# A two-layer graph network on one NeuronCore: layer 1 entered tile by tile, its weights prepared during layer 0's experts, key and value scales moved to the context

## The chip, the cores and the metric

One Trainium2 chip, one of its NeuronCores. The metric is device time in microseconds of one execution, median of the runs. A profiled execution of the same program gives busy times, waits and the granted TensorE clock; it is longer than the plain runs, and its own time is given beside its span.

## The reference, cut to what matters

There are 3125 nodes of 256 features and 50,000 edges sorted by destination. Each of two layers adds to the node features x a graph branch and a mixer branch, both computed from the layer norm of x, and then an expert branch. Layer 0 ends with eight experts of which each node uses two. Layer 1 is:

```python
xn = _layernorm(x)
x = x + gnn1(xn) + mix1(xn)
x = x + ffn1(_layernorm(x))

# mix1, with heads of 32 features
q, k, v = split((xn @ w_qkv + b_qkv) by head)
k = _ln(k, kln_g, kln_b)
v = _ln(v, vln_g, vln_b)
kv = einsum('nhd,nhe->hde', k, v) / 3125
h = gelu((einsum('nhd,hde->nhe', q, kv) + xn) @ w1 + b1)
mix1 = h @ w2 + b2 + xn

# gnn1: mean of xn[src] over the edges of each node
o = concat([xn, agg]) @ weight
gnn1 = o / norm(o) + bias

# ffn1: softmax router over 8 experts, all used; each is
# relu(bn(x W1 + b1)), relu(bn(h W2 + b2)), h Wo + bo
```

All of it is float32.

## The kernel before, in words

The nodes lie in 25 tiles of 128 rows (the last has 53). X (L345) holds all of them in SBUF. Instructions are put in order by a scheduler which starts from the order of the program; each engine then works its own queue strictly in that order. Four kinds of PSUM tile exist, "tr", "mm", "acc" and "seg", with two buffers each (L195).

*Layer 0's experts* (L944 to L973) run over 32 slots of 256 gathered rows. A slot loads its expert's two weights and its rows on SP's DMA queue, transposes, multiplies twice with Gelu between, and writes its result to the DRAM table yex from ScalarE's queue. From slot 8 on, every third slot also issues the loads of one layer-1 expert's three weights (L970).

*Layer 1's beginning* (L978 to L1056). Once the loop is over, the pool lp is opened, the mixer's and the graph branch's weights and seven rows of constants are loaded, and three things are prepared on VectorE: the key and value weights lose their head means (hm, L1001 to L1006, so that keys and values come out centred), the query weights are transposed (wqT), and m_b2 is added to g_bias. Then chunks of four tiles (L1014) are entered: eight gathers from yex on POOL, two weighted adds per tile into X (L1025), layer norm statistics, the normalizing on VectorE (L1030), two transposes, a copy into xT (L1034), a product with half of g_w (L1036) whose result goes to the DRAM table xtab (L1038), and two VectorE instructions that add the normed rows and g_bias to X (L1039, L1040). The edge gathers of layer 1 read xtab and can start once the whole table is stored.

*The mixer* (mixer1, L1062). Per tile: keys and values by a 128x512 product, offset added (L1071), Square on ScalarE, sum by head (L1074), Sqrt on ScalarE, reciprocal, multiplication by the inverse deviation (L1077), by kvln_g (L1079), addition of kvln_b (L1080), and two products that accumulate the context in the two "acc" buffers (L1083). After 25 tiles the diagonal blocks go to cb, are multiplied into w1 and the query weights (L1094 to L1107), and seven chunks of tiles, last tiles first (BACK: six of four tiles and one of one), get the mixer's output added to X.

*The experts of layer 1* (L1154). For each chunk of BACK: route (layer norm, transposes, router, softmax, bias product), then eight experts of two products with Relu and a third product added to X. Routing of the next chunk is begun beside expert 3 or later of the present chunk, if the edge sums of its tiles are complete.

*Order written by hand* (L1262 to L1276). The generator other() yields units of expected TensorE time: 3.7 per tile of keys and values, 6.0 for the context, 0.85 per tile and product pair after that. The 49 groups of eight edge blocks are inserted in between: group g when 14 + 11.5 g units have passed, or at once where an expert chunk waits for them. A group builds a one-hot tile on VectorE (L290), sums eight blocks of 128 edges with one product each (L1241), spreads the sums over node tiles (L1254 to L1258) and, where a node tile is complete, closes it (aggregate, L1196 to L1210), which needs an "acc" buffer.

Of the kernel before, what the change touches and what calls it, by code (L numbers as in the profile page):

```python
# [8 lines left out]
F32 = mybir.dt.float32  # L9
I32 = mybir.dt.int32  # L10
AF = mybir.ActivationFunctionType
ALU = mybir.AluOpType
# [175 lines left out]
def fast_path(ctx: ExitStack, tc: tile.TileContext, i, out, ident, dstP):  # L188
# [750 lines left out]
    fW = [fw.tile([Q, NE, KC, D], F32, name=f"fw_{n}", tag=f"fw_{n}") for n in ("f_W1", "f_W2", "f_Wo")]  # L939
    with ExitStack() as l0e:  # L940
# [3 lines left out]
        for k in range(MT):  # L944
# [24 lines left out]
            nc.scalar.dma_start(yex[k * ME:(k + 1) * ME, :].rearrange("(j p) c -> p j c", p=Q), yo)  # L969
            if k >= 8 and k % 3 == 2 and (k - 8) // 3 < NE:  # L970
                e = (k - 8) // 3
                for w, name in zip(fW, ("f_W1", "f_W2", "f_Wo")):
                    nc.sync.dma_start(w[:, e], i[name][e].rearrange("(k p) c -> p k c", p=Q))  # L973
# [4 lines left out]
    lp = ctx.enter_context(tc.tile_pool(name="lp", bufs=1))  # L978
    wk = ctx.enter_context(tc.tile_pool(name="wk", bufs=2))

    def weights(name, n, k=KC):
        t = lp.tile([Q, k, n], F32, name=f"w_{name}", tag=f"w_{name}")
        nc.sync.dma_start(t, i[name].rearrange("(k p) c -> p k c", p=Q))
        return t

    wqkv = weights("m_wqkv", 3 * D)
    w1 = weights("m_w1", D)
    w2 = weights("m_w2", D)
    wg = weights("g_w", D, 2 * KC)
    wr = weights("f_Wr", NE)  # L990
    fbo = lp.tile([NE, D], F32, name="fbo", tag="fbo")
    nc.sync.dma_start(fbo, i["f_bo"])
    br = row_load(lp, "br")
    kvb = row_load(lp, "kv_b")
    lng = row_load(lp, "kvln_g").rearrange("p (s d) -> p s d", s=2)
    lnb = row_load(lp, "kvln_b").rearrange("p (s d) -> p s d", s=2)
    gb = row_load(lp, "g_bias")
    mb2 = row_load(lp, "m_b2")
    nc.vector.tensor_tensor(gb, gb, mb2, ALU.add)

    hm = lp.tile([Q, KC + 1, 2 * NH], F32, name="hm", tag="hm")  # L1001
    for k in range(KC + 1):
        w = (wqkv[:, k, D:3 * D] if k < KC else kvb).rearrange("p (h d) -> p h d", d=DH)
        nc.vector.tensor_reduce(hm[:, k, :], w, AX.X, ALU.add)
        nc.vector.tensor_scalar(hm[:, k, :], hm[:, k, :], 1.0 / DH, None, op0=ALU.mult)
        nc.vector.tensor_tensor(w, w, bc(hm[:, k, :], 2, DH), ALU.subtract)  # L1006

    wqT = lp.tile([Q, KC, D], F32, name="wqT", tag="wqT")
    for k in range(KC):
        pt = transposed(wqkv[:, k, 0:D])  # L1010
        nc.vector.tensor_copy(wqT[:, :, k * Q:(k + 1) * Q], pt)
    xT = lp.tile([Q, KC, NT, Q], F32, name="xnT", tag="xnT")
    xtab = dram.tile([NPAD, D], F32, name="xtab", tag="xtab")
    for t0, n in CHUNKS:  # L1014
        xs = X[:, t0:t0 + n, :]
        for k in range(2):
            ye = wk.tile([Q, 4, D], F32, name="ye", tag="c4", bufs=7)
            for j in range(n):
                r = rows(t0 + j)
                nc.gpsimd.indirect_dma_start(  # L1020
                    out=ye[0:r, j, :], out_offset=None, in_=yex[:, :],
                    in_offset=bass.IndirectOffsetOnAxis(ap=slot[0:r, k, t0 + j:t0 + j + 1], axis=0))
            for j in range(n):
                r = rows(t0 + j)
                nc.vector.scalar_tensor_tensor(X[0:r, t0 + j, :], ye[0:r, j, :], gate[0:r, k, t0 + j:t0 + j + 1],  # L1025
                                               X[0:r, t0 + j, :], op0=ALU.mult, op1=ALU.add)
        mv, rs = ln_stats(xs, n)
        xn = wk.tile([Q, 4, D], F32, name="xn", tag="c4", bufs=7)
        for j in range(n):
            normed(xn[:, j, :], xs[:, j, :], mv, rs, j)  # L1030
        yt = wk.tile([Q, 4, D], F32, name="yt", tag="c4", bufs=7)
        for j in range(n):
            pt = transposed(xn[:, j, :])
            nc.scalar.copy(xT[:, :, t0 + j, :], pt)  # L1034
            py = ps("seg", [Q, D])
            product(py, [xT[:, k, t0 + j, :] for k in range(KC)], [wg[:, KC + k, :] for k in range(KC)])  # L1036
            nc.scalar.copy(yt[:, j, :], py)
        nc.sync.dma_start(xtab[t0 * Q:(t0 + n) * Q, :].rearrange("(t p) c -> p t c", p=Q), yt[:, 0:n, :])  # L1038
        nc.vector.tensor_tensor(xs, xs, xn[:, 0:n, :], ALU.add)  # L1039
        nc.vector.tensor_tensor(xs, xs, bc(gb, 1, n), ALU.add)  # L1040
# [4 lines left out]

    bn = []
    for s in ("1", "2"):
        g = lp.tile([Q, NE * KC], F32, name=f"bn_s{s}", tag=f"bn_s{s}")
        nc.scalar.activation(g, cols_of("f_v" + s), AF.Sqrt, bias=eps3)
        nc.vector.reciprocal(g, g)  # L1050
        nc.vector.tensor_tensor(g, g, cols_of("f_g" + s), ALU.mult)
        b = lp.tile([Q, NE * KC], F32, name=f"bn_b{s}", tag=f"bn_b{s}")
        nc.vector.tensor_tensor(b, cols_of("f_b" + s), cols_of("f_m" + s), ALU.subtract)
        nc.vector.tensor_tensor(b, b, g, ALU.mult)
        nc.vector.tensor_tensor(b, b, cols_of("f_be" + s), ALU.add)
        bn.append((g, b))  # L1056


    BACK = [list(range(t, max(-1, t - 4), -1)) for t in range(NT - 1, -1, -4)]
    complete = set()  # L1060

    def mixer1():  # L1062

        cx = [ps("acc", [Q, Q]) for _ in range(2)]
        for t in range(NT):
            pm = ps("mm", [Q, 2 * D])
            product(pm, [xT[:, k, t, :] for k in range(KC)], [wqkv[:, k, D:3 * D] for k in range(KC)])
            ks = c4("kv").rearrange("p s (h d) -> p s h d", d=DH)
            kv, sq = ks[:, 0], ks[:, 1]
            kf = kv.rearrange("p h d -> p (h d)")  # L1070
            nc.vector.tensor_tensor(kf, pm, kvb, ALU.add)  # L1071
            nc.scalar.activation(sq, kv, AF.Square)
            va = wk.tile([Q, 2 * NH], F32, name="va", tag="va")
            nc.vector.tensor_reduce(va, sq, AX.X, ALU.add)  # L1074
            nc.scalar.activation(va, va, AF.Sqrt, bias=eps5, scale=1.0 / DH)
            nc.vector.reciprocal(va, va)
            nc.vector.tensor_tensor(kv, kv, bc(va, 2, DH), ALU.mult)  # L1077
            k4 = kv.rearrange("p (s h) d -> p s h d", s=2)
            nc.vector.tensor_tensor(k4, k4, bc(lng, 2, NH), ALU.mult)  # L1079
            nc.vector.tensor_tensor(k4, k4, bc(lnb, 2, NH), ALU.add)  # L1080
            r = rows(t)
            for a in range(2):
                nc.tensor.matmul(cx[a], kf[0:r, D + a * 128:D + (a + 1) * 128], kf[0:r, a * 128:(a + 1) * 128],  # L1083
                                 start=(t == 0), stop=(t == NT - 1))
            yield 3.7
# [907 lines left out]
```

## Time and profile before

| | |
|---|---|
| Median of 3 runs | 2813.36 us (2812.88 to 2814.0) |
| Profiled execution | 2967.99 us, span 2966.2, mean granted clock 0.945 |
| PE | 2640.8 us busy, 89% of the span |
| DVE (VectorE) | 1517.6 us, 51% |
| POOL | 917.0 us, 31% |
| ACT (ScalarE) | 873.5 us, 29% |
| HBM | 160.14 MB read, 53.61 MB written |
| Chain that ended last | PE 79%, DVE 10%, unknown queue 4%, issue 3% |

PE is TensorE, PEld its weight loads, DVE VectorE, ACT ScalarE. One float32 product appears as two MATMUL instructions. Busy time of an engine is the sum of its instructions; idle time of an engine matters only where others wait for it. In a row of instruction groups one reads line, engine, operation, output and inputs, shapes, count, then busy microseconds and mean nanoseconds, then the engine's idle time just before such instructions and what ended it. "Remote", or an unknown queue, is a wait whose end no engine or data transfer in the trace accounts for.

### The profile page before, as it was taken

The page shows a single profiled execution, that of the slowest core. Times are in us where ns is not written, and L with a number is a line of the kernel's source. Part 1 is how long each engine was busy: PE and PEld are TensorE (multiplying, and loading weights), DVE is VectorE, ACT ScalarE, POOL GpSimd, SP SyncE. Part 2 cuts the span into 40 slices and gives each one's busy share as a digit, 9 for nine tenths or more (in the row PEclk, how much of TensorE's full clock was granted, in tenths as well). Part 3 has the DMA queues.
Part 4 walks back from the last instruction along what each step waited for, and adds up shares of the span by engine and source line. Part 5 has one row for each costly group of instructions (what it writes and reads, how often), then busy time and mean ns, then how long its engine had stood idle before and what let it go on. Part 6 is the DMA issues. An engine that isn't in the chain of part 4 may idle for free.

```text
span 2966.2 us, 29959 instructions
## 1 busy us (share of the span) xinstructions
PE 2640.8 (89%) x10578; PEld 1891.9 (64%) x10578; DVE 1517.6 (51%) x3749; ACT 873.5 (29%) x1621; POOL 917.0 (31%) x964
## 2 busy tenths in 40 slices
PE   5899989989988779898998699856789999999998
PEld 4666768656676457686665588734556666666655
DVE  6376655856657557668556311176834333322211
ACT  3432225312252112343333122222233222322223
POOL 2107542144521335200122100065354544555200
PEclk9899999999999889999998799978889999999999
DMA  4002221022212121100111576442122222222100
GB/s 141 12 16 89 81 90 38 22 77 76 86 47 70 29 77 41 59 4 13 31 58 59 191 252 200 153 145 81 47 75 64 75 67 71 71 73 78 33 8 10
DMA packets 152337, 215.85 MB, mean 73 GB/s; under 512 B 21032, under 2 KB 120686, under 8 KB 152178
## 3 DMA queue, kind: packets, MB, share of 16 engines
q1 hardware_dynamic: 104274, 112.31, 11.7%
q0 software_dynamic: 36848, 91.34, 10.8%
q10 hardware_dynamic: 11056, 10.19, 1.1%
q8 instruction: 86, 1.41, 0.2%
q14 instruction: 73, 0.60, 0.1%
HBM read 160.14 MB, written 53.61 MB: 72 GB/s over the span
## 4 chain that ended last, share of the span: by engine, by line
PE 79%; DVE 10%; another core or an unknown queue 4%; issue 3%; ACT 2%; DMA 1%; POOL 0%; SPq 0%; DVEq 0%; ACTq 0%
PE mm L280 33%; PE acc L280 24%; PE seg L467 6%; PE seg L1241 6%; PE acc L614 3%; PE tr L274 3%; PE seg L280 1%; PE acc L335 1%; DVE vals L457 1%; DVE gt L422 1%; DVE st L521 1%; DMA raw<-in_src 0%; PE tr L280 0%; DVE hT L737 0%
## 5 line engine op out<-in xcount | busy, mean ns | idle before, releaser
L283 POOL DMA_INDIRECT gt<-table,srcI x391 | 426.9, 1092 | 807.1 <-DVE m L425 602.9
L283 POOL DMA_INDIRECT gt<-xtab,srcI x391 | 381.7, 976 | 394.8 <-PE seg L1241 241.9
L280 PE MATMUL mm<-hT,w 128*128 128x512 f32 (+2 forms) x896 | 381.7, 562 | 23.7 <-ACT gT L688 16.2
L280 PE MATMUL acc<-w,gT 128*128 128x256 f32 x1600 | 370.0, 387 | 6.2 <-issue 4.2
L280 PEld LDWEIGHTS acc<-w,gT 128*128 128x128 f32 x1600 | 306.4, 194 | 53.1 <-issue 6.9
L1182 ACT ACTIVATE fh<-mm,bn_b,bn_s 128x512 f32<-128x512 f32 (+1 forms) x224 | 163.1, 731 | 425.8 <-PE mm L280 391.9
L280 PEld LDWEIGHTS mm<-hT,w 128*128 128x128 f32 x896 | 164.5, 193 | 158.8 <-issue 100.0
L339 DVE SCALAR_TENSOR_TENSOR X<-acc,rw,X 128x256 f32<-128x256 f32 x200 | 95.1, 483 | 325.9 <-PE acc L280 277.2
L688 ACT ACTIVATE gT<-mm,cols 128x512 f32<-128x512 f32 (+2 forms) x224 | 142.3, 641 | 354.0 <-PE mm L280 263.5
L280 PE MATMUL mm<-wqkv,hT 128*128 128x256 f32 x800 | 214.2, 399 | 15.6 <-ACT hT L723 9.0
L467 PE MATMUL seg<-vals,oh 128*128 128x261 f32 x782 | 192.0, 399 | 13.3 <-DVE oh L290 8.7
L280 PE MATMUL acc<-fw_f_Wo,fh 128*128 128x256 f32 x800 | 198.4, 385 | 1.6 <-issue 0.7
L280 PE MATMUL mm<-fh,fw_f_W 128*128 128x512 f32 (+1 forms) x448 | 195.3, 565 | 1.6 <-ACT fh L1182 1.3
L1241 PE MATMUL seg<-gt,oh 128*128 128x256 f32 x782 | 186.6, 388 | 3.8 <-DVE sum L1258 2.7
L280 PE MATMUL mm<-xc,fw_f_W 128*128 128x512 f32 (+1 forms) x448 | 188.9, 551 | 0.0
L467 PEld LDWEIGHTS seg<-vals,oh 128*128 128x128 f32 x782 | 152.9, 198 | 52.8 <-DVE oh L290 15.7
L280 PEld LDWEIGHTS acc<-fw_f_Wo,fh 128*128 128x128 f32 x800 | 144.7, 190 | 59.1 <-issue 27.9
L1241 PEld LDWEIGHTS seg<-gt,oh 128*128 128x128 f32 x782 | 150.4, 194 | 38.5 <-issue 12.8
L280 PEld LDWEIGHTS mm<-wqkv,hT 128*128 128x128 f32 x800 | 144.2, 197 | 40.4 <-ACT K L566 11.4
L699 DVE TENSOR_TENSOR X<-acc,X 128x256 f32<-128x256 f32 x100 | 42.2, 422 | 220.8 <-PE acc L280 149.2
L1020 POOL DMA_INDIRECT ye<-yex,slot x50 | 51.5, 1030 | 297.4 <-DVE cb L1087 273.8
L280 PEld LDWEIGHTS mm<-fh,fw_f_W 128*128 128x128 f32 x448 | 78.2, 191 | 99.5 <-issue 68.7
(329 smaller groups left out, 3877.0 us busy)
## 6 DMA issues: line engine op xcount, KB each, us to landing
ew<-in_e_W SPq DMA_DIRECT2D x64, 512.0 KB
tok<-zero SPq DMA_DIRECT2D x8, 3328.0 KB
w<-in_W SPq DMA_DIRECT2D x8, 1024.0 KB
hr<-tok SPq DMA_DIRECT2D x32, 256.0 KB
yex<-yo ACTq DMA_DIRECT2D x32, 256.0 KB
gt<-table,srcI POOLq DMA_INDIRECT x391
gt<-xtab,srcI POOLq DMA_INDIRECT x391
fw_f_W<-in_f_W SPq DMA_DIRECT2D x16, 256.0 KB
```

The costliest lines, as they stand in the source:

```text
L274: nc.tensor.transpose(pt[:, k, :], src_row[:, k * Q:(k + 1) * Q], ident)
L280: nc.tensor.matmul(pm, a, b, start=(k == 0), stop=(k == len(lhs) - 1))
L283: nc.gpsimd.indirect_dma_start(out=dst, out_offset=None, in_=tab[:, :], in_offset=bass.IndirectOffsetOnAxis(ap=srcI[:, b:b + 1], axis=0))
L335: nc.tensor.matmul(py, cT[:, j, :], bt, start=True, stop=True)
L339: nc.vector.scalar_tensor_tensor(X[:, t, :], py, cw, X[:, t, :], op0=ALU.mult, op1=ALU.add)
L467: nc.tensor.matmul(open_seg[w_], oh[:, b - h0, :], v[:, b - h0, :], start=(b == a), stop=(b == z))
L614: nc.tensor.matmul(cx[a], K[0:r, t, a * 128:(a + 1) * 128], keys.hn[0:r, t, :], start=(t == 0), stop=(t == NT - 1))
L688: nc.scalar.activation(gT[:, f, :], pm, AF.Gelu, bias=col("b1", l * NF + f))
L699: nc.vector.tensor_tensor(X[:, t, :], py, X[:, t, :], ALU.add)
L1020: nc.gpsimd.indirect_dma_start(out=ye[0:r, j, :], out_offset=None, in_=yex[:, :], in_offset=bass.IndirectOffsetOnAxis(ap=slot[0:r, k, t0 + ...
L1182: nc.scalar.activation(hn[:, a, 0:w], pm, AF.Relu, bias=bn[s][1][:, c:c + 1], scale=bn[s][0][:, c:c + 1])
L1241: nc.tensor.matmul(segs[w], oh[:, j, :], gt[:, j, :], start=(b == z), stop=(b == a))
```

## The change

- Pool lp is opened before the expert loop. The loads and preparations of layer 1's weights become a generator, layer1_weights, advanced at slots 9, 12, 15, 18 and 21 of the expert loop.
- The beginning goes tile by tile. Gathers of both expert results of a tile stand together, in groups of 2, 3 and then 4 tiles; three groups are fetched ahead, and the buffers are those that the edge gathers use later. The tile's adds run four tiles ahead. Both uses of the normalization go to ScalarE: xn, and X + xn as one scaled and shifted copy of X. The addition of g_bias goes to the mixer's output chunks.
- Of the 28 steps of keys and values, 18 are issued among the entries of tiles (three for every four tiles).
- kvln_g and kvln_b no longer touch the keys and values. Scaled values and keys go to a ring of three buffers with a column of ones; the context products give sums of the values beside the context, and one more product with ones per tile gives sums of the keys. At the end scale, offset and their cross terms are applied to the 128x128 context by means of four prepared tiles (cf).
- A remaining step of keys and values counts 2.5 units instead of 3.7.
- BACK becomes four chunks of four tiles and three of three.

```diff
+    def layer1_weights():
+        w = {}
+        w["qkv"] = weights("m_wqkv", 3 * D)
+        w["kvb"] = row_load(lp, "kv_b")
...
+        yield w
...
+    l1w, ready = None, layer1_weights()
...
+            if k >= 9 and k % 3 == 0:
+                l1w = next(ready, l1w)
...
+    BACK = [list(range(t, t - 4, -1)) for t in range(NT - 1, 8, -4)] + [list(range(t, t - 3, -1)) for t in (8, 5, 2)]
...
+    def add_y(t):
...
+        for k in range(2):
+            nc.vector.scalar_tensor_tensor(X[0:r, t, :], yes[g][0:r, 2 * (t - t0) + k, :], gate[0:r, k, t:t + 1],
+                                           X[0:r, t, :], op0=ALU.mult, op1=ALU.add)
+        st = stat.tile([Q, 6], F32, name="st", tag="st", bufs=4)
+        nc.vector.bn_stats(st, X[:, t, :])
+        nc.vector.bn_aggr(mvx[:, t, :], st)
+        if t == t0 + n - 1:
...
+            fetch_y(g + 3)
+    def norm_y(t):
+        xn = wk.tile([Q, D], F32, name="xn", tag="h", bufs=2)
+        nc.scalar.activation(xn, X[:, t, :], AF.Identity, scale=rsx[:, 0, t:t + 1], bias=rsx[:, 1, t:t + 1])
+        pt = transposed(xn)
+        nc.scalar.copy(xT[:, :, t, :], pt)
+        nc.scalar.activation(X[:, t, :], X[:, t, :], AF.Identity, scale=rsx[:, 2, t:t + 1], bias=rsx[:, 1, t:t + 1])
...
+    def keys_values():
+        cx = [ps("acc", [Q, Q + 1]) for _ in range(2)]
+        ks = ps("seg", [Q, 2, Q + 1])
+        def sums(t):
+            kv, r = kvs[t % 3], rows(t)
+            se = dict(start=(t == 0), stop=(t == NT - 1))
+            for a in range(2):
+                nc.tensor.matmul(cx[a], kv[0:r, 2 + a, 0:Q], kv[0:r, a, :], **se)
+            nc.tensor.matmul(ks.rearrange("p a c -> p (a c)"), ones[0:r, :], kv[0:r, 0:2, :].rearrange("p a c -> p (a c)"),
+                             **se)
...
+                nc.vector.tensor_tensor(kvs[t % 3][:, :, 0:Q].rearrange("p g (h d) -> p g h d", d=DH),
+                                        kv.rearrange("p (g h) d -> p g h d", g=4),
+                                        bc(va, 2, DH).rearrange("p (g h) d -> p g h d", g=4), ALU.mult)
+            if t >= 2:
+                sums(t - 2)
+            yield
...
+    AHEAD = 4
+    for t in range(AHEAD):
+        add_y(t)
+    norm_y(0)
+    kvsteps, due = keys_values(), 0
+    for t in range(NT):
+        if t + AHEAD < NT:
+            add_y(t + AHEAD)
+        if t + 1 < NT:
+            norm_y(t + 1)
+        product_y(t)
+        while due < 0.75 * t - 0.5:
+            next(kvsteps)
+            due += 1
+    norms_of_experts()
 
     def mixer1():
...
-            nc.vector.tensor_tensor(kv, kv, bc(va, 2, DH), ALU.mult)
-            k4 = kv.rearrange("p (s h) d -> p s h d", s=2)
-            nc.vector.tensor_tensor(k4, k4, bc(lng, 2, NH), ALU.mult)
-            nc.vector.tensor_tensor(k4, k4, bc(lnb, 2, NH), ALU.add)
...
-            yield 3.7
...
+        for _ in kvsteps:
+            yield 2.5
+        cb = contexts[0]
...
             gT = c4("gT1")
+            nc.vector.tensor_tensor(X[:, t0:t0 + n, :], X[:, t0:t0 + n, :], bc(l1w["gb"], 1, n), ALU.add)
```

The products that product_y issues are those of L1036, unchanged. The two instructions per expert norm at L1046 to L1056 become norms_of_experts, after the last tile is entered.

## The prediction

> **What bounds the kernel now.** I read the stages first: busy time, granted clock and DMA share in five stretches. The borders are the last expert result of layer 0 written out (1921.2), the last node tile entering layer 1 (about 2011, its table row stored at 2011.3) and the end of the key-value context (2126). Columns: stretch, length, busy us of PE, PEld, DVE, ACT, POOL (instructions), PEclk, DMA share, GB/s.
> ```profile
> 1680.00:1921.00 241.00, 228.00 (x1091) 194.78 (x1089) 39.16 (x61) 56.91 (x120) 0.00 (x0) 1.00 0.65 211
> 1921.00:2014.00 93.00, 50.97 (x170) 34.12 (x171) 66.24 (x177) 23.20 (x65) 51.71 (x51) 0.78 0.44 134
> 2014.00:2126.00 112.00, 76.30 (x252) 45.59 (x252) 86.89 (x166) 23.39 (x51) 55.74 (x56) 0.85 0.23 66
> 2200.00:2966.00 766.00, 754.09 (x2705) 481.36 (x2703) 234.33 (x520) 220.81 (x348) 286.44 (x295) 0.99 0.19 55
> ```
> Before and after layer 1's beginning TensorE is 95 to 98% busy at full clock. In the 205 us between, it is busy 127 and at a clock of 0.78 to 0.85, while VectorE is busy 153: this is the stretch that the change rewrites, and VectorE holds it. Second, the groups of instructions of 1921.9 to 2126 by form, the costliest of VectorE:
> ```profile
> L1025 DVE SCALAR_TENSOR_TENSOR X<-ye,gate,X 128x256 f32<-128x256 f32 x48 | 20.0, 475 | 7.5 <-issue 7.5
> L1080 DVE TENSOR_TENSOR kv<-kv,r_kvln_b 128x512 f32<-128x512 f32 x25 | 17.2, 687 | 0.0
> L1077 DVE TENSOR_TENSOR kv<-kv,va 128x512 f32<-128x512 f32 x25 | 17.0, 682 | 0.1
> L1079 DVE TENSOR_TENSOR kv<-kv,r_kvln_g 128x512 f32<-128x512 f32 x25 | 16.8, 671 | 0.0
> L1071 DVE TENSOR_TENSOR kv<-mm,r_kv_b 128x512 f32<-128x512 f32 x25 | 16.7, 669 | 19.1 <-remote 10.9 <-PE mm L280 8.2
> L1074 DVE TENSOR_REDUCE va<-kv 128x16 f32<-128x512 f32 x25 | 16.5, 670 | 1.3 <-ACT kv L1072 1.3
> L268 DVE TENSOR_SCALAR xn<-X,mv,rs 128x256 f32<-128x256 f32 x25 | 8.8, 414 | 0.2
> L1039 DVE TENSOR_TENSOR X<-X,xn 128x1024 f32<-128x1024 f32 x6 | 7.4, 1225 | 0.2
> L1040 DVE TENSOR_TENSOR X<-X,r_g_bias 128x1024 f32<-128x1024 f32 x6 | 7.3, 1224 | 0.2
> ```
> Five of these nine (L1080, L1079, L268, L1039, L1040) are instructions that the change takes from VectorE here. Third, the timeline of the first VectorE work on layer 1:
> ```profile
> 1920.49 0.69 DVE L968 COPY yo<-acc 128x512 f32<-128x512 f32 x1 [6.51 <-PE acc L280]
> ...
> 1931.46 0.88 DVE L1025 SCALAR_TENSOR_TENSOR X<-ye,gate,X 128x256 f32<-128x256 f32 x2 [7.46 <-issue]
> ```
> The first gather is issued at 1924.16 and the chain of waits gives it 6.16 us to land, beside 2.4 MB of weights and rows; TensorE transposes the first tile only at 1942.4, after eight gathers and the weight preparation.
>
> **VectorE in the stretch.** Leaves: L1079 and L1080, 25 x (0.671 + 0.687) = 34 us; L268, 8.8; L1039 and L1040 with their one-tile forms, 15.6; weight preparation (hm, wqT, offsets, L999 to L1011), about 6. That is 64 of 153. Stays, per tile: two adds 0.95, statistics 0.40, aggregate 0.17, key-value work 0.669 + 0.670 + 0.244 + 0.682 = 2.27; 3.8 x 25 = 95. With the deviations (7 groups of 0.5), two one-hot builds of 1.22, some six sums of 0.48, the norms of the experts (2) and the new context work (twelve small operations, about 3.6), 109 us.
>
> **TensorE in the stretch.** Per tile at full-clock durations of the timeline: transposes 0.30, product for the table 1.00, keys and values 1.85, context 0.65. New is a product with ones, 128x258, two instructions per tile; its nearest row is L1241 (128x256), 16 instructions in 3.62, so 0.45. Sum 4.25 x 25 = 106. The hand-written order now lets 10 x 2.5 + 6 units pass to the context's end where it let 98.5, so two groups of edge sums (16 blocks) stand ahead of it; 16 x 0.45 = 7. In all 113: TensorE and VectorE become level. What clock? The Trainium skill (TensorE: Matmul & The Clock Gate, Part 1) says that the clock halves only after an idle window of about 3.4 us and is full again after as long a busy one; gaps that short waits leave would then cost nothing and the work stays 113. The rows show 0.85 in the key-value stretch although its last 66 us have few such gaps. I take the row, since the mutual waits of two level engines remain: 113/0.85 = 133.
>
> **ScalarE.** Two normalizing ACTIVATEs per tile are new. The nearest row, L1201 (one pointer operand), is 508 ns; the skill's rule against the move (ScalarE: Activation LUTs, What ACT_TABLE_LOAD costs) is 280 ns + 0.833 ns per element, and 93 for a second pointer: 586, dearer than the 414 and 306 they replace. With the two copies (0.37 each), Square (0.63) and Sqrt (0.31) that is 2.9 us a tile by the rule, 2.7 by the row, 72 or 68 in all: under 133 either way, so off the path. Between zero and 5 us for longer chains; I take zero, inside the 0.85.
>
> **The lead-in and POOL.** The first gathers still wait for the last expert result (landed 1923.4). Gathers now come tile by tile at 1.25 us each, so two tiles have landed by about 1931 and TensorE starts near 1933: 12 us after 1921.2. POOL supplies a tile per 2.5 us, less than the 4.25/0.85 = 5.0 that a tile with its keys and values takes. If DMA latency stays at 6 us the lead is 3 more; if it falls to 2, 1 less. Three groups (nine tiles) are fetched ahead, so POOL, waiting for a buffer behind VectorE's adds, delays nobody; the queue behind it is only the edge gathers, which wait for the last table store anyway.
>
> **Sum of the stretch.** 12 + 133 + 4 for the longer end of the context = 149, against 2126.0 - 1921.2 = 205: 56 gained. Of the 205, 15 are waits on an unknown queue (10.90 and 4.34 the two long ones), which I leave where they are: they may go (-8) or grow (+5).
>
> **What is given back, and smaller things.**
> - *Edge sums.* 66 instructions (33 blocks) ran before 2126; now 16 blocks. Seventeen blocks x 0.45 = +7.7, on a TensorE that is 98% busy.
> - *The last chunk.* The last edge group is due at 14 + 48 x 11.5 = 566 units in both kernels. The whole was 705.5 units and is now 638, of which the last three tiles' experts take 68. So their routing can no longer begin beside the chunk ahead. Chain after the last block by rows: sum 0.48, L1201 0.51, L1202 0.42, square 0.42, table load 1.28, 0.20, 0.16, L1210 0.48, statistics and scale about 1.0, norm 0.41, transposes 0.3, copy 0.37, two more tiles 0.8, ten hops of 0.2: 8.9. The chunk's last product covers 2.6, a restart at half clock costs about 2: +8, between 3 and 14.
> - *Chunks.* 6 x 4 + 1 tiles become 4 x 4 + 3 x 3. An expert takes 10.87 us for four tiles and 3.61 for one, so 8 x (6 x 10.87 + 3.61) = 551. For three, 8 x (3 x 8.2 + 4 x 10.87) = 545 if 8.2 scales as the matmuls do; -5, between -6 and +2.
> - *Offsets g_bias* (7 x 1.22 on VectorE) go to the mixer chunks, where VectorE is about 45% busy, later 31%: hidden, 8.5 if that cover were gone; +1.
> - *Weights among the experts.* Six DMAs on SP (0.37 each, SP idle), seven row loads on ScalarE's queue (about 0.5 each, ScalarE 24% busy), some 9 us of VectorE (16% busy, 6.5 us idle between copies) and six transposes: they hide unless something ahead in an in-order queue waits. +2, between 0 and 15.
>
> Sum: -56 + 7.7 + 8 - 5 + 1 + 2 = -42 of the profiled execution's own 2967.99, so 2926. The median of the plain runs is 2813.36, 0.948 of it; the gain in that ratio is 40: **2773 us**.
>
> **Rivals.** (B) *Full clock and close packing*: the rule above holds, TensorE needs 113, the gain in the stretch is 76 and the total -62 x 0.948 = -59: 2754. For it: VectorE was 95% busy from 2060 to 2126, so the order is packed well. Against it: one more engine at its limit. (C) *Waits take the place of work*: VectorE's queue is in order, so an add that waits for a gather holds back key-value steps, and those wait for ScalarE twice a tile (Square, Sqrt); the stretch then gains only 25, total -11: 2803. For it: 10.9 and 8.2 idle before L1071. (D) *The expert loop stalls, slower*: in the first experts DMA already runs at
> ```profile
> 1680.00:1760.00 80.00, 75.95 (x366) 65.06 (x365) 12.89 (x20) 18.97 (x40) 0.00 (x0) 1.00 0.84 275
> ```
> that is, 52 GB/s are left of 327. The 2.4 MB need 46 us of that; if VectorE's preparing instructions stand in its queue ahead of the experts' copies (hTe, yo) and wait all that time, TensorE waits too, with 9 us of preparation on the path and three restarts at the clock of 0.76 that 1660 to 1680 shows (4.8 each): 46 + 9 + 14 - 2 = 67 more than above, x 0.948: 2837. It ends slower from the point where the experts lose 42 us. For it: the loads come from memory that is busiest just there. Against it: TensorE is 95% busy at that share, no weight is wanted for three experts after its issue, and the share falls to 0.62 after 1760. (E) *It moves nothing*: the scheduler puts key-value steps after all gathers as now, and only the preparation's 10 us are won, eaten by the 13 given back: 2813.
>
> **How the numbers follow.** Likeliest (0.55) 2773, its own range 2752 to 2792; B 0.20, 2754, reaching to 2740; C 0.14, 2803; E 0.05, 2813; D 0.06, 2837. The range from 2742 to 2800 leaves out D, E and part of B and C. A measurement of this kernel can tell about 0.2%, 5.6 us, from no change: faster is A, B and C (0.89), same E (0.05), slower D (0.06).
>
> **What would show it.** Right: L1079 and L1080 gone; from the last layer-0 result to the first product with the context about 150 us, with TensorE's busy share there from 62% to near 80% and a clock of 0.85 or more; the first transposes some 12 us after the last result; 16 blocks of edge sums before the context's end; a gap of 5 to 10 us before the last three tiles' experts; the expert loop within 5 us of its present length. Wrong: if the stretch has TensorE waiting for VectorE's adds (C), if the experts' loop grows by tens of us with VectorE waiting for a DMA (D), if VectorE's durations rise when ScalarE and POOL are busier, or if the gap before the last chunk is not there or far longer.

## The result, and the profile after

| | before | after |
|---|---|---|
| Median, five runs each | 2813.36 us (2811.32 to 2814.0) | 2778.97 us (2773.83 to 2783.72) |
| Ratio to before, 95% interval | | 0.9882 (0.9866 to 0.9898) |
| Profiled execution | 2967.99 us | 2780.31 us, span 2778.5 |

34 us less; 2773 was forecast. The experiments came in sessions of two kinds, "short" (the kernel before takes 2814 us) and "long" (2989 to 2994), so each kernel's time is compared with that of the kernel before of its own session, and traces only with traces of a like session. A profiled execution is not longer as such: that of the kernel after (2780.31) is one of its five runs. That of the kernel before (2968) is of the long kind by its length and by the waits in it; no profile of before from a short session exists.

Three stretches of the profile after: layer 0's experts, the stretch (last expert result of layer 0 issued, to the result of the first product with the context), and all that follows. Columns as in the prediction: stretch, length, busy PE, PEld, DVE, ACT, POOL, PEclk, DMA share, GB/s.
```profile
1565.70:1811.20 245.50, 232.67 (x1116) 198.94 (x1114) 44.54 (x76) 58.69 (x124) 0.00 (x0) 1.00 0.69 220
1811.20:1947.30 136.10, 104.94 (x422) 68.91 (x422) 97.65 (x244) 66.38 (x163) 71.43 (x69) 0.89 0.31 91
1947.30:2778.50 831.20, 813.91 (x2957) 537.24 (x2957) 277.85 (x624) 245.10 (x392) 367.87 (x372) 0.99 0.22 63
```
The stretch has 136 us; VectorE does 98 us in it, where it did 155 (in a long session; the first experiment has the row); TensorE's share is 77%. The expert loop has kept its 245.5 us. The groups of the stretch (line, engine, operation, then busy, mean ns, idle before and what ended it):
```profile
L1094 DVE SCALAR_TENSOR_TENSOR X<-ye,gate,X 128x256 f32<-128x256 f32 x48 | 22.3, 472 | 18.8 <-DMA ye<-yex,slot 18.7
L1150 DVE TENSOR_TENSOR kvs<-kv,va 128x512 f32<-128x512 f32 x25 | 17.0, 682 | 0.3
L1113 ACT ACTIVATE X<-X,rsx 128x256 f32<-128x256 f32 x25 | 14.9, 601 | 0.1
L1110 ACT ACTIVATE xn<-X,rsx 128x256 f32<-128x256 f32 x25 | 14.7, 597 | 9.4 <-DVE mvx L1098 4.8 <-DVE rsx L1103 4.5
L1135 PE MATMUL seg<-kvs,ones 128*128 128x258 f32 x48 | 14.5, 383 | 0.0
L1217 DVE TENSOR_TENSOR X<-X,r_g_bias 128x1024 f32<-128x1024 f32 x3 | 3.6, 1202 | 0.1
```
L1079 and L1080 of before are gone, and nothing like them is there. New is VectorE's wait for gathers, 18.7 us ahead of L1094. The last row is not where the program has it: the additions of g_bias stand in the mixer's chunks, but the scheduler put six of the seven (with the three of 128x768, 6.3 us) into the stretch.

The beginning of the stretch, timeline of the kernel after (last result issued at 1811.2):
```profile
1824.67 0.29 ACT L1101 ACTIVATE rsx<-mvx,eps 128x2 f32<-128x2 f32 x1 [11.78 <-DVE mvx L1098]
...
1828.43 0.15 DVE L1102 RECIPROCAL rsx<-rsx 128x2 f32<-128x2 f32 x1
...
1829.78 1.09 ACT L1110 ACTIVATE xn<-X,rsx 128x256 f32<-128x256 f32 x2 [4.82 <-DVE mvx L1098]
...
1830.43 1.18 PE L274 MATMUL tr<-ident,xn 128*128 128x128 f32 x4 [19.98 <-ACT xn L1110]
```
The deviations' root is done at 1824.96, their reciprocal runs 3.5 us later. No semaphore ended that time: between the two, VectorE's queue holds adds of tiles 3 and 4, each waiting for its gather. And the last three tiles, after the last group of edge sums:
```profile
2690.04 2.80 PE L280 MATMUL acc<-fw_f_Wo,fh 128*128 128x256 f32 x12
...
2696.49 0.73 PE L274 MATMUL tr<-ident,hs 128*128 128x128 f32 x4 [3.65 <-DVE hs L268]
...
2697.69 2.47 PE L280 MATMUL tr<-w_f_Wr,xc 128*128 128x8 f32 x12
```
TensorE stands still 3.65 us and soon after works at half clock (from 2698.0 for 6.8 us): from the end of the products at 2692.84 to the experts' first product at 2700.0 are 7.2 us.

### The profile page after: what moved, and what is told of

Read it like the earlier page. It is cut to its first block, busy times and chain, and to the rows that moved or that the text cites. A ratio compares the mean times of both kernels' runs of the same rounds, so it can differ in the third digit from the quotient of the medians.

```text
span 2778.5 us, 29986 instructions
## 1 busy us (share of the span) xinstructions
PE 2596.7 (93%) x10630; PEld 1884.7 (68%) x10630; DVE 1480.8 (53%) x3704; ACT 897.0 (32%) x1672; POOL 935.6 (34%) x964
## 5 line engine op out<-in xcount | busy, mean ns | idle before, releaser
L283 POOL DMA_INDIRECT gt<-table,srcI x391 | 439.5, 1124 | 689.4 <-DVE m L425 495.9
L467 PE MATMUL seg<-vals,oh 128*128 128x261 f32 x782 | 183.7, 387 | 3.7 <-DVE vals L457 3.7
L280 PE MATMUL mm<-hTe,ew 128*128 128x256 f32 x512 | 123.9, 391 | 12.0 <-DVE hTe L1021 12.0
## 6 DMA issues: line engine op xcount, KB each, us to landing
tok<-zero SPq DMA_DIRECT2D x8, 3328.0 KB, 12.7
```

Of the source, the lines that this page charges most:

```text
L280: nc.tensor.matmul(pm, a, b, start=(k == 0), stop=(k == len(lhs) - 1))
L283: nc.gpsimd.indirect_dma_start(out=dst, out_offset=None, in_=tab[:, :], in_offset=bass.IndirectOffsetOnAxis(ap=srcI[:, b:b + 1], axis=0))
L467: nc.tensor.matmul(open_seg[w_], oh[:, b - h0, :], v[:, b - h0, :], start=(b == a), stop=(b == z))
```

## Experiments

**The kernel before, profiled again**

> The kernel before, unchanged, profiled once more, because its first profiled execution (2968 us) was 155 us longer than its plain runs. If the unknown-queue waits of the first profile (10.9 and 4.3 us in the stretch from the last layer-0 result to the first context product) belong to that execution alone, this one is near 2813 us and the stretch some 190 us instead of 205, with a clock above 0.85 in it. If they belong to the kernel, the profile is again near 2960 and the stretch 205. After the change the stretch measures 135 us.

It took 2995.86 us, a single run in a long session. Stretch and rest:
```profile
1947.60:2159.10 211.50, 130.03 (x436) 83.41 (x437) 155.10 (x348) 48.46 (x120) 109.21 (x106) 0.80 0.32 94
2159.10:2994.00 834.90, 809.00 (x2899) 520.63 (x2897) 265.42 (x605) 243.89 (x388) 327.17 (x335) 0.98 0.20 57
```
So the 2968 us of the first profile were no accident of one execution; the kernel is that long in every run of the long sessions. The stretch is that of the first profile too (210.1 to this end; the prediction's 205 ended at the finished context, 5 us earlier). For a short session this much can be said: the four profiles of such sessions have the last expert result at 1810.0 to 1813.4, in code that the change leaves alone but for the weights. If before has it at 1811.2 too, then the 2813.4 - 1.8 - 1811.2 = 1000 us of before that follow became 967. How they divide into stretch and rest was not measured.

**The kernel after, again**

> The kernel after, unchanged, timed again beside the kernel before. On the chip of the first experiments all kernels take some 177 us longer than in the first comparison (before 2990 instead of 2813 us), with places where TensorE, VectorE and ScalarE stand still together. If these places cost both kernels the same, the ratio to before is 1 - 34/2990 = 0.9885 on that chip and 0.988 on the first one; if the change meets fewer or more of them, the ratio there differs by 0.003 or more.

2950.41 us against 2994.12, ratio 0.986 (0.9844 to 0.9875), in a long session: the same gain within the intervals. Stretch and rest:
```profile
1927.10:2106.40 179.30, 109.67 (x422) 71.95 (x422) 97.62 (x243) 65.81 (x163) 75.82 (x77) 0.79 0.25 75
2106.40:2939.50 833.10, 813.07 (x2957) 536.21 (x2957) 278.05 (x624) 245.31 (x392) 363.38 (x365) 0.99 0.21 62
```
The same 422 products take 179 us here and 136 in the short session. The difference is that of three waits of TensorE, of 15.2, 9.3 and 18.4 us; the first, in the timeline:
```profile
1960.49 0.44 PE L274 MATMUL tr<-ident,xn 128*128 128x128 f32 x2 [1.25 <-ACT xn L1110]
...
1967.11 0.95 POOL L1084 DMA_INDIRECT ye<-yex,slot  x1 [0.30 <-issue]
1968.36 0.95 POOL L1084 DMA_INDIRECT ye<-yex,slot  x1 [0.30 <-issue]
1969.61 0.94 POOL L1084 DMA_INDIRECT ye<-yex,slot  x1 [0.30 <-issue]
...
1975.68 0.37 ACT L1112 COPY xnT<-tr 128x256 f32<-128x256 f32 x1 [14.57 <-remote]
...
1976.11 1.22 PE L280 MATMUL seg<-w_g_w,xnT 128*128 128x256 f32 x2 [15.18 <-issue]
```
ScalarE's copy needs the transposes, which ended at 1960.9, and starts at 1975.7; all the while POOL issues one gather per 1.25 us. Over the whole trace, behind its first 15 us, there are ten places where TensorE, VectorE and ScalarE stand still together for over 3.5 us (3.9 to 16.8, 73 us in all); each begins inside a run of gathers issued less than 2.3 us apart, of which 10 to 40 had gone before. In the profile of the short session there is none, though its runs of gathers are as long.

The two long traces of before and after also differ where the change does nothing: the last expert result is out at 1947.6 in the one and at 1927.1 in the other. Over all long sessions it varies from 1921.2 to 1947.6.

**Scales and offsets back on the tiles**

```diff
+                nc.vector.tensor_tensor(k4, k4, bc(l1w["lng"], 2, NH), ALU.mult)
+                nc.vector.tensor_tensor(k4, k4, bc(l1w["lnb"], 2, NH), ALU.add)
...
-            nc.tensor.matmul(ks..., ones[0:r, :], kv[0:r, 0:2, :]...)
...
```


> The kernel after, with kvln_g and kvln_b put back on each tile's keys and values (two 128x512 VectorE instructions of 0.68 us per tile) and the product with ones and the cross terms taken out. Theory of the prediction (TensorE and VectorE are level in the stretch): VectorE gets 34 us more in a stretch in which it is 75 per cent busy, its tail tiles go from 2.3 to 3.7 us of VectorE against 2.6 us of TensorE; the stretch grows by 16 to 26 us, total about 2800 us. Rival (TensorE alone bounds it, VectorE only fills gaps): the removed product with ones gives back 10 to 14 us of TensorE and the total is 2766 to 2782.

2963.07 against 2990.11, ratio 0.9908 (0.9884 to 0.9931): against the kernel after's 0.986, 14 us longer, uncertain by some 8 (the two half intervals, 0.0023 and 0.0016, as root of squares, of 2990 us; the same below). Stretch:
```profile
1937.10:2125.60 188.50, 109.77 (x373) 65.89 (x374) 122.68 (x289) 66.48 (x161) 82.23 (x82) 0.77 0.25 75
```
25 us more work of VectorE cost 9 us of stretch, though 49 of TensorE's instructions are gone. The theory has the sign, but not its 16 to 26 us; the rival, that VectorE only fills gaps, is out.

**Norms on VectorE**

```diff
-        nc.scalar.activation(xn, X[:, t, :], AF.Identity, scale=rsx[:, 0, t:t + 1], bias=rsx[:, 1, t:t + 1])
+        nc.vector.tensor_scalar(xn, X[:, t, :], rsx[:, 0, t:t + 1], rsx[:, 1, t:t + 1], op0=ALU.mult, op1=ALU.add)
```
and the same for the second one.

> The kernel after, with both normalizing steps of a tile on VectorE instead of ScalarE: 50 instructions of about 0.41 us, 20 us, all among the entries of tiles, where VectorE is 66 of 86 us busy. Theory (VectorE is level with TensorE there): 5 to 15 us longer, about 2789 us. Rival (a tile's chain of latencies bounds the entry, ScalarE's 0.6 us per step counts): 0 to 6 us shorter, about 2776 us.

2958.02, ratio 0.9897 (0.9873 to 0.992): 11 us longer than the kernel after, by 8 uncertain; the trace gives 3 us in the stretch (182.2 against 179.3). VectorE's load matters a little there too; the rival's gain is not there.

**Keys and values after the entries**

```diff
-        while due < 0.75 * t - 0.5:
+        while due < 0:
```


> The kernel after, with all 28 key-value steps behind the entries of tiles in the program's order instead of 18 among them. Theory (the gathers, 50 x 1.25 us on POOL, pace the entry, and the steps fill TensorE meanwhile): the entries end near 1884 instead of 1911, then 25 tiles at 2.6 us follow, context at about 1955 to 1960 instead of 1946, so 8 to 14 us longer there; against it some five more groups of edge sums pass before the context (moved, not added) and the last chunk's routing is no longer late (7 us back): total 2775 to 2790. Rival (the interleaving is what gains the time, since TensorE's work in the entry is only 33 us of 70): 20 to 30 us longer, about 2805 us.

2970.66, ratio 0.9937 (0.9914 to 0.996): 23 us longer. Stretch and rest:
```profile
1934.40:2150.40 216.00, 133.75 (x500) 87.56 (x500) 110.23 (x269) 72.76 (x174) 101.44 (x102) 0.80 0.26 77
2150.40:2971.60 821.20, 796.22 (x2879) 520.71 (x2879) 265.06 (x599) 247.93 (x386) 334.76 (x340) 0.99 0.20 59
```
37 us longer before the context, 12 shorter behind it: 78 more of TensorE's products have passed ahead (five groups of edge sums instead of one). In such a session the interleaving is worth 23 of the 42 us (0.014 of 2990) that the whole change gains, as the rival said; the expected early end of the entries came (last copy into xT 103 us after the last result, against 125), but did not pay.

**Weights after the loop**

```diff
-            if k >= 9 and k % 3 == 0:
-                l1w = next(ready, l1w)
...
+    for l1w in ready:
+        pass
```


> The kernel after, with layer 1's weights loaded and prepared only when the expert loop is over. Theory (the prediction's 10 us of preparation lay on the path, and 2 us of cost in the loop): the loads, 2.4 MB, and the preparation stand ahead of the first gathers' adds on VectorE and ahead of the first products on TensorE; 8 to 18 us longer than the kernel after. Rival (the lead is set by the expert result's landing, the gathers and the deviations, 19 us, behind which the loads hide): 0 to 5 us longer, or up to 3 shorter since the expert loop is relieved.

2948.85, ratio 0.9849 (0.9832 to 0.9865), 3 us below the kernel after and within its interval; stretch 180.1 against 179.3, loop 245.3 against 245.6. The rival holds: loads and preparation hide behind the wait for the first tile, and making them early gains nothing that can be told with this entry.

**Edge sums every 11 units**

```diff
-    spent, g, PACE, FROM = 0.0, 0, 11.5, 14.0
+    spent, g, PACE, FROM = 0.0, 0, 11.0, 14.0
```


> The kernel after, with groups of edge sums due every 11.0 units instead of 11.5, so that the last group is due at 542 units, ahead of the fourth expert of the last chunk but one, instead of 566. Theory (the prediction's step of +8 for the late routing of the last three tiles is real: the profile after shows 3.65 us of idle TensorE and half clock there): the gap goes, 5 to 9 us shorter than the kernel after. Rival (the gap is only moved: the groups now press earlier, where gathers or the experts' chains wait for them): 0 to 3 us shorter, or longer by up to 5.

2950.28, ratio 0.9861 (0.9845 to 0.9876): no change. In the trace the gap before the last tiles is gone (the longest wait of TensorE behind the context is 2.65 us) and the rest is 1.6 us shorter; the stretch is 3.8 longer, with a second group of edge sums (32 instead of 16 instructions) ahead of the context. Moved, not won.

**Adds behind the first deviations**

```diff
+    last = next(x for x in reversed(nc.cur_bb.bb.instructions) if x.engine == nc.vector.engine)
+    with tc.issue_after(last):
+        add_y(2)
+    add_y(3)
```


> The kernel after, with the adds of the third and later tiles queued on VectorE behind the deviations of the first two tiles. In the profile after, ScalarE's Sqrt is done at 1825.0, but the reciprocal stands behind adds that wait for their gathers, and runs at 1828.4; the first transposes come 19 us after the last expert result instead of the predicted 12. Theory (that order costs the lead 3 to 4 us, and the lead is on the path): 2 to 4 us shorter. Rival (the entry is paced by the gathers on POOL, which run on at 1.25 us each anyway): no change, within 1 us.

2943.85, ratio 0.9848 (0.9823 to 0.9872): no change that can be told, and no test either. Only tile 2 was held; the adds of tiles 3 and 4 took its place ahead of the reciprocal, and the first copy into xT came 21.2 us after the last result instead of 20.1. The question was put again in the last experiment.

**Short runs of gathers**

```diff
-    ENT = [(0, 2), (2, 3)] + [(t, 4) for t in range(5, NT, 4)]
+    ENT = [(t, min(2, NT - t)) for t in range(0, NT, 2)]
...
-        xn = wk.tile([Q, D], F32, name="xn", tag="h", bufs=2)
+        xn = yes[g][:, 2 * (t - ENT[g][0]), :]
...
+        if t == sum(ENT[g]) - 1:
+            fetch_y(g + 3)
```


> The kernel after, with the entry's gathers in groups of two tiles (four gathers), and ScalarE's normalized tile written into the group's own buffer, so that POOL gathers a group only after TensorE has transposed the tiles of three groups before: after the first twelve gathers POOL's unbroken run of 50 becomes runs of four. The profile of the kernel after on the second chip shows three places in its stretch (15.2, 9.3 and 18.4 us) where TensorE waits though its inputs are made, each inside an unbroken run of gathers, 21 to 40 of them long. Theory (the unbroken run of gathers is what holds the other engines up): on that chip the first two go, 15 to 25 us shorter than the kernel after, the third, inside the edge gathers, stays. Rival 1 (the places belong to the instructions, not to POOL): they stay, the time is unchanged or up to 8 us longer because gathers come later. On the first chip, whose profile shows none of these places, both expect 0 to 8 us longer.

In a short session: 2776.63 against 2813.94, ratio 0.9874 (0.9858 to 0.989), the kernel after's time within the interval. The stretch is 7 us shorter (129.1), the rest 3.6 longer (834.8). The runs did not become runs of four: the trace has 12, 12, 8, 8, 4, 4 and 2 gathers less than 2.3 us apart. A short session has none of the places that the theory speaks of, so it can't decide here.

**Chunks of before**

```diff
-    BACK = [list(range(t, t - 4, -1)) for t in range(NT - 1, 8, -4)] + [list(range(t, t - 3, -1)) for t in (8, 5, 2)]
+    BACK = [list(range(t, max(-1, t - 4), -1)) for t in range(NT - 1, -1, -4)]
```


> The kernel after, with the chunks of the kernel before (six of four tiles and one of one instead of four of four and three of three). The prediction put the change of chunks at 5 us gained (between 6 gained and 2 lost), from 8.2 us for an expert of three tiles, 10.87 of four and 3.61 of one. Theory: 3 to 6 us longer than the kernel after in the part behind the context (833 us there). Rival (the late routing costs more with three tiles than with one, and the order of edge sums was made for either): unchanged or up to 5 us shorter.

2771.86 against 2813.94, ratio 0.9854 (0.9839 to 0.987), 8 us below the kernel after's ratio, by 6 uncertain. Stretch and rest:
```profile
1813.40:1948.10 134.70, 104.77 (x422) 69.15 (x422) 97.64 (x244) 66.63 (x163) 70.13 (x69) 0.89 0.31 92
1948.10:2771.20 823.10, 811.05 (x2957) 527.70 (x2957) 278.25 (x624) 245.40 (x393) 365.66 (x372) 1.00 0.22 64
```
The rest is 8.1 us shorter with as many products, and the late routing's wait is not there: tile 0 alone is routed beside the experts of tiles 4 to 1. The theory (3 to 6 us longer) is wrong; the gap of the last tiles comes with the change of chunks.

**Plain loads in place of the gathers**

```diff
-                    nc.gpsimd.indirect_dma_start(out=yes[g][0:r, 2 * j + k, :], out_offset=None, in_=yex[:, :], ...)
+                    nc.sync.dma_start(yes[g][0:r, 2 * j + k, :], yex[(MT - 1) * ME:(MT - 1) * ME + r, :])
```


> The kernel after, with the entry's 50 gathers replaced by 50 plain loads from the last expert result, issued from SP (every tile gets the same rows: the weighted adds stay, the rows that they should add are left out). POOL is then idle in the entry. Theory (POOL's gathers pace the entry, and on the second chip their unbroken run holds the other engines up): on that chip the stretch loses its two places of 15 and 9 us and the pacing of 2.5 us a tile, 30 to 40 us shorter than the kernel after; on the first chip 8 to 15 us shorter, because TensorE, 104 us busy in the stretch, then stands still for little but the lead. Rival (deviations, ScalarE and VectorE pace the entry): 0 to 10 us shorter on either.

2755.79, ratio 0.9802 (0.9786 to 0.9817), in the short session: 23 us below the kernel after. Stretch:
```profile
1810.80:1924.00 113.20, 100.72 (x422) 67.75 (x422) 95.52 (x243) 65.49 (x163) 19.20 (x19) 0.94 0.36 109
```
All of it lies in the stretch, and TensorE, VectorE and ScalarE have as many instructions there as in the kernel after. TensorE's first transposes come 11.6 us after the last result instead of 19.2. VectorE's waits for rows ahead of the weighted adds, 21.2 us in the kernel after, are 0.9. More than the 8 to 15 expected. The run takes away POOL's issuing, the gathers' landing and their place in VectorE's queue at once, and reads the same rows again and again; it shows what the gathers cost together, not each part.

**All that pointed the right way, together**

```diff
+    with tc.issue_after(last):
+        add_y(2)
+        add_y(3)
...
+            with tc.issue_after(last) if t < 6 else contextlib.nullcontext():
+                add_y(t + AHEAD)
...
+            with queued():
+                nc.vector.tensor_tensor(X[:, t0:t0 + n, :], X[:, t0:t0 + n, :], bc(l1w["gb"], 1, n), ALU.add)
```
with the entry of the short runs and the chunks of before.

> What the experiments point to, together: the kernel after with the entry of the short-bursts experiment, the chunks of the kernel before, the adds of tiles 2 to 9 queued on VectorE behind the first deviations (this time all of them), and the additions of g_bias queued behind what stands before them, so that they stay in the mixer's chunks. Theory, if the parts add up: 7 us from the chunks, 2 from the entry, 3 from the lead, 2 to 4 from the seven additions of 1.22 us: 14 to 16 us less than the kernel after, ratio to the kernel before 0.983 where that takes 2814 us (2764 to 2768). Rival (they overlap: the entry is paced by the gathers on POOL, 50 x 1.25 us, whatever VectorE does): 8 to 10 us less, ratio 0.985. On the chip where the kernel before takes 2990 us and the stretch has its unbroken run of gathers, the theory of the runs expects 15 to 25 us more to go (ratio 0.976), the rival that the places stay (0.983).

In a long session: 2915.47 against 2988.65, ratio 0.9752 (0.9725 to 0.9779), 32 us less than the kernel after by the ratios (9 uncertain) and 73 less than before: the fastest of all kernels there. Stretch and rest:
```profile
1928.20:2081.30 153.10, 109.28 (x422) 70.72 (x422) 95.21 (x256) 68.29 (x169) 75.97 (x77) 0.87 0.30 88
2081.30:2909.60 828.30, 812.46 (x2957) 527.46 (x2957) 283.41 (x630) 245.19 (x393) 361.95 (x364) 1.00 0.21 62
```
The beginning, where root and reciprocal now stand together:
```profile
1939.66 0.29 ACT L1102 ACTIVATE rsx<-mvx,eps 128x2 f32<-128x2 f32 x1 [9.78 <-DVE st L1098]
1939.99 0.17 DVE L1103 RECIPROCAL rsx<-rsx 128x2 f32<-128x2 f32 x1 [0.36 <-ACT rsx L1102]
...
1941.17 1.18 PE L275 MATMUL tr<-ident,ye 128*128 128x128 f32 x4 [13.72 <-issue]
```
The transposes begin 13.0 us after the last result, 6 earlier; with the short runs alone they began 19.3 us after it. The longest run of gathers in the entry is now 16, no longer 42 and 8. The places of 15.2 and 9.3 us among the entry's gathers are gone (the longest wait there is now 4.6 us); the third, among the edge gathers, whose runs were left as they are, stands there with 4.4 and 12.7. This is what the theory of the runs expected, to the place. It isn't a proof of the runs alone: the adds' order and g_bias were changed with them, and long sessions differ among themselves. The rest is 4.8 us shorter. How much of it holds in a short session wasn't tried.

## Why the prediction came out right, step by step

The total is right (34 us gained, 40 forecast; by the medians of the long session 44 of 2994, where the sum had 42 of 2968), but several terms are wrong and cancel, so that it comes so near is in part luck.

- **VectorE holds the stretch: half right.** Its work fell from 155 us to 98 (153 and 109 forecast), and putting the scales back costs 14 us, by 8 uncertain. But that was for 25 us more of VectorE's work, and the gathers cost more (23 us).
- **"POOL ... delays nobody": the step that failed.** Without gathers the same work is 23 us shorter. The prediction compared rates (2.5 us a tile against 5.0) and left out the order: adds that wait for gathers stand in VectorE's in-order queue ahead of deviations and key-value steps. That is rival C's mechanism, in part. After the first deviations the second ones show it, up to TensorE:
```profile
1831.52 0.30 ACT L1101 ACTIVATE rsx<-mvx,eps 128x3 f32<-128x3 f32 x1
...
1835.81 0.48 DVE L1094 SCALAR_TENSOR_TENSOR X<-ye,gate,X 128x256 f32<-128x256 f32 x1 [2.30 <-DMA ye<-yex,slot]
...
1836.55 0.16 DVE L1102 RECIPROCAL rsx<-rsx 128x3 f32<-128x3 f32 x1
...
1837.78 0.69 PE L274 MATMUL tr<-ident,xn 128*128 128x128 f32 x2 [4.03 <-ACT xn L1110]
```
  The root is done at 1831.82 and its reciprocal runs 4.7 us later, behind adds; at the third deviations it is 2.9 us.
- **The lead of 12 us was 19.2.** The 12 is what the plain loads show (11.6) and nearly what the last experiment shows (13.0). The rows came as forecast (the fourth one's add starts 10.3 us after the last result; the prediction had two tiles landed 10 us after it); with the adds behind the deviations 6 of the 7 us are gone, so these were the order of VectorE's queue, not the gathers' latency, for which the prediction had allowed 3.
- **The clock: full where TensorE was kept busy; 0.85 was too low.** The prediction weighed 113 us at full clock, by the Trainium skill (TensorE: Matmul & The Clock Gate, Part 1), against 133 by the row of 0.85, and took the row. From the first transposes to the context product are 116 us in the short session, with one group of edge sums (8 blocks) ahead where two were forecast, 120 with the second. Two parts of that time, in the profile after:
```profile
1825.00:1911.00 86.00, 69.50 (x275) 45.76 (x276) 65.59 (x177) 52.20 (x131) 44.10 (x42) 0.89 0.33 97
1911.00:1946.50 35.50, 34.74 (x146) 22.85 (x144) 26.27 (x54) 12.29 (x30) 18.50 (x19) 1.00 0.26 78
```
  In the last 35 us TensorE is 98% busy at 1.00; the 0.89 before it has the start after 20 us of idleness in it and two waits of 4.0 and 3.4 us. The row of 0.85 had waits for VectorE in it, which the change removes: in the first profile, the 66 us that the prediction says have "few such gaps" hold this wait,
```profile
2063.39 1.22 PE L1083 MATMUL acc<-kv 128*128 128x128 f32 x4 [5.02 <-DVE kv L1080]
```
  with half clock from 2062.2 on, and two more phases at half clock (from 2099.75 and from 2116.82). The 3.4 us before each of these two, and full clock between:
```profile
2069.03:2099.75 30.72, 26.12 (x102) 16.19 (x101) 30.32 (x56) 7.11 (x16) 16.53 (x17) 1.00 0.24 70
2096.34:2099.75 3.41, 1.28 (x7) 0.88 (x8) 3.35 (x6) 0.08 (x1) 2.58 (x3) 1.00 0.34 95
2113.41:2116.82 3.41, 0.98 (x7) 0.60 (x5) 3.41 (x7) 0.11 (x1) 0.00 (x0) 1.00 0.00 0
```
  No single wait there is above 2.1 us, but TensorE was busy for only 1.3 and 1.0 of 3.4 us. So the prediction's reading of the rule, that short waits cost nothing, does not hold in this trace: several close together were followed by half clock. Rival B, which took full clock, put the stretch at 205 - 76 = 129, closer to the short session's 136 than 149 is; in the long session it took 179.
- **Scaling by 0.948** took the session's extra time for an even stretching. It isn't: of the 161 us between the two profiles of the kernel after, 116 lie ahead of the stretch, 43 in it and 2 behind it, and within the stretch they sit in three waits of TensorE. In the long session the stretch fell by 32 us where 56 was forecast, and what follows fell by 2 where it was to grow by 12; before has one of the places (a wait of TensorE of 7.6 us) behind its context, the kernel after has its last (18.4) ahead of it. Another 20 us by which the two long traces differ lie ahead of the stretch and are not the change's.
- **Late routing +8, chunks -5: sizes right and wrong, and one cause.** The wait with its half clock is 7.2 to 8 us. But it takes the three-tile chunk that needs the last group's tile as well as the late group: with the chunks of before it isn't there, with the groups due as late, and neither is it with groups every 11 units. The 5 us gained by chunks did not come; together +8 (by 6 uncertain) where +3 was forecast. A chunk edit was costed by its products alone, without asking when its tiles are complete.
- **Edge sums displaced:** 25 blocks, 11 us at 0.45, where 17 and 7.7 were forecast; the second group that 31 units allow was put behind the context.
- **Product with ones:** 0.60 us for two instructions on the timeline, not 0.45; 4 us more in all. **ScalarE:** 597 and 601 ns; the 586 estimated from the Trainium skill (ScalarE: Activation LUTs, What ACT_TABLE_LOAD costs) was right within 3% and the row's 508 low. Neither decided.
- **g_bias:** 6.3 of the 8.5 us came into the stretch; the step followed the program and not the scheduler. Its price alone wasn't measured.
- **Weights:** the loop is unchanged (245.5 us, +2 forecast, rival D's 42 us out), but the 6 us of preparation weren't on the path either.
- **Rival E** is out with the ratio; its placing of the key-value steps behind the entries costs 23 us in the experiment that does it, and still leaves a gain on before (ratio 0.9937).

What stays open: what makes a session long, and why the engines stand still inside runs of gathers there. It isn't the chip alone: the record has the same chip number for the short session of the last three single experiments and for the long one of all together. It may even be the recording: every profile of a long session holds some 18,000 records of semaphore changes where one of a short session holds 28,000, so records are lost there, some "remote" waits may have an ender that wasn't recorded, and no run tells whether what loses the records also holds the engines. Open is also how before's 1000 us divide between stretch and rest in a short session.

## What to carry to other kernels

A rate that is low enough is not cover: ask in which in-order queue the consumer of a gather waits, and what stands behind it. Where a profiled execution is longer than the plain runs, find the places that make the difference before a sum is made on it; a mean clock below one comes of waits, here of 5.0 us and of several near 2 us close together, so ask whether the change leaves them before carrying the clock over. And when chunks are cut anew, cost the moment at which each chunk's inputs are complete with the products.

## What the runs showed of the hardware

The same program took 2814 us in two sessions and 2989 to 2994 in three, with the same durations of most instructions (379 and 592 ns are the medians of the same products in both). In the two profiles of the kernel after, TensorE is 33 us longer busy and 128 us longer idle in the long session; the longest idle times are ten places where three engines stand still together while POOL issues gathers without a gap (73 us in all, none in the short session), from 10 gathers in a run on. With the entry's runs of 42 and 8 broken up into runs of at most 16, and the other edits of the last experiment, both of its places were gone. POOL issues a gather every 1.25 us in either kind of session. TensorE's clock fell to half after 3.4 us in which it was busy for 1.0 to 1.3 us, and stayed full over 35 us in which it was 98% busy.
